# Macaron attention on one core: the order of the work beside the first unit's maxima, and beside the last heads' copies

## The chip, the core and the metric

The kernel runs on one core of a Trainium2 chip. The metric is the device time of one execution in microseconds (us), and the median over the runs is taken. The engines are called as in the profile: PE multiplies matrices, PEld is its weight load, DVE, ACT and POOL work on vectors, and SP issues most of the DMAs. All data is float32.

## What is computed

The input x has 8 batches of 1024 tokens with 256 features. The reference is a macaron block:

```
x = x + 0.5 * ffn(layernorm(x))
x = x + attn(layernorm(x))
x = x + 0.5 * ffn(layernorm(x))
```

`attn` is causal attention with 16 heads of 16 features: q, k and v are projections with biases, the scores q·k/4 get a causal mask and a softmax, and the weighted values go through the output projection Wo with bias bo. `ffn` sends each token to its two best of 8 experts, and an expert that is asked by more tokens than its capacity (1280 of 8192 tokens, where 2048 are the mean) gives nothing to anyone. The kernel counts the tokens of each expert, proves that none is kept, and runs a feed-forward path only if a count says otherwise. The trace shows no instruction of that path, so with these inputs both feed-forward layers add zero. What the time consists of is therefore the attention of 8 batches, the gate logits of both layers, the choice of two experts for each token, and the counts.

## The kernel before

**Units.** `attention` (from line 681 on) cuts the work into 32 units: unit u is batch u // 4 with group u % 4 of four heads. The four heads lie on partitions 0, 32, 64 and 96 of four rotating pairs of tiles qT and kT. The softmax is done in two passes. `m_steps(u)` multiplies q and k of unit u block by block (PE writes PSUM tiles named sm) and takes row maxima on DVE. `settle(u, hf)` sends the maxima of one half of the rows through DRAM (top_d) into row 16 of each head in qT, against a row of -1 in kT, so that the second multiplication comes out with the maximum already subtracted. `e_steps(u)` does that second multiplication (PSUM tiles sc), ACT takes the exponential into pT, POOL cuts the diagonal blocks, and PE multiplies by the values into pav. Six PSUM tiles serve sm and sc in rotation (`score`), and two more (`bank`) serve everything else.

**The main loop.** For u from -1 to 31 the loop does 24 steps. For u from 0 to 30, a step is two blocks of sc of unit u and two blocks of sm of unit u+1, and then the value products that are owed from earlier steps. For u = -1 there are no scores yet: 12 pairs of steps do only the maxima of unit 0, four blocks each. In the text P1 to P12 are these pairs, 512, 384, 256 and 128 columns wide in P1 to P4 and in P9 to P12, and 512 in P5 to P8.

**Work beside it.** All else is written as generators and handed to an object `Beside` (line 52). A generator yields PIECE before a piece of PE work, REST before the second half of a piece, or a number of steps to wait. `beside.step(True)` moves the clock on by one step, runs what is due, and then runs the open second half or opens one PIECE. So one call gives PE about half a piece of other work behind a step. `finish` runs a generator to its end at once. In the opening (u = -1) one `step` is called behind each pair. The order in which the Python calls are made is the order on each engine, since `InOrder` (line 27) chains the instructions of PE, DVE, ACT and POOL. SP's DMAs are not chained by it.

The generators that matter here:
- `weights` (line 215): turns the weight matrices with PE transposes, one piece for each of wk, wq, the gate, wv and wo. Then it centres the gate's weights (three DVE operations on gsb to gcs), turns them (pt_gc), multiplies them with bo and Wo (pg), and multiplies the bias of v by Wo (pb_v), whose result DVE adds to bo_all. Two copies on POOL, bo_cols and bv_cols, serve these products.
- `values_of(b, apart, j0, j1)`: a tile of v for 128 tokens in two halves (pv), copied by ACT to vaug and by DVE to the logits.
- `project(u, apart)`: q and k of units u and u+1, in four pieces of two halves (pq), one for each of k and q in each half of the tokens. ACT writes packed, and SP spreads it with 8 DMAs a piece, 32 in all, one for each head.
- `residual`, `gate_first`, `prepare`, `enter`: the residual with its bias on POOL, the first layer's choice of experts on DVE, and the next batch's layer norm.
- `leave_last(b, hf, pav, copies)`: the last four heads of the last batch. Two copies bring pav to SBUF (att_last), PE transposes, DVE divides (normed), PE transposes back (on_last), two copies follow, and four px_last products end it. `regate` then computes the second layer's logits and its choice of experts, about 20 small DVE operations, and `fewest` counts.

**Order around the change, before.** In the opening: the gate and wv behind P1, and values of tiles 0 to 3, half a tile behind each of P3 to P10. Nothing is left for P11 and P12. In unit 0, one half behind each step: values of tiles 4 to 7 (steps 0 to 7), `project(2)` (steps 8 to 15), then the rest of `weights`, then `residual(0)` and `gate_first(0)`. At the end, after the last unit: `finish` runs everything that is pending, which is the rest of the first half's `regate`, then the first layer's count, and only then `leave_last` for the second half.

Of the kernel before, what the change touches and what calls it, by code (L numbers as in the profile page):

```python
# [10 lines left out]
F32 = mybir.dt.float32  # L11
# [7 lines left out]
P = 128  # L19
# [29 lines left out]
PIECE, REST = "piece", "rest"  # L49
# [51 lines left out]
def macaron_kernel(  # L101
# [22 lines left out]
    DC = D // P  # L124
# [90 lines left out]
    def weights(pool, bank, matmul, transpose):  # L215
        def load(src, queue):
            wsb = pool.tile([P, DC, D], F32, tag="wsb", name="wsb", bufs=4)
            queue.dma_start(out=wsb, in_=src.rearrange("(c p) d -> p c d", p=P))
            return wsb

        wks, wqs = load(Wkv[:D], nc.scalar), load(Wq, nc.scalar)
        with nc.allow_non_contiguous_dma(reason="two vectors of 256"):
            for src, dst in ((bkv[:D], bkT), (bq, bqT)):
                nc.scalar.dma_start(out=dst, in_=src.rearrange("(c p) -> p c", p=P))
        gsb = const.tile([E, D], F32, name="gsb")
        nc.sync.dma_start(out=gsb, in_=gate_w)
        wvs, wos = load(Wkv[D:], nc.sync), load(Wo, nc.sync)
        nc.sync.dma_start(out=bo_all[:, :D], in_=bo.partition_broadcast(P))
        boT = const.tile([P, DC], F32, name="boT")
        bvT = const.tile([P, DC], F32, name="bvT")  # L230
        with nc.allow_non_contiguous_dma(reason="two vectors of 256"):
            nc.sync.dma_start(out=boT, in_=bo.rearrange("(c p) -> p c", p=P))
            nc.sync.dma_start(out=bvT, in_=bkv[D:].rearrange("(c p) -> p c", p=P))

        gpsimd.tensor_scalar(bqT, bqT, QSCALE, None, ALU.mult)

        def turn(wsb, dst):
            pt = bank("pt_w")
            for kc in range(DC):
                for oc in range(DC):  # L240
                    transpose(pt[:, kc * D + oc * P : kc * D + (oc + 1) * P], wsb[:, oc, kc * P : (kc + 1) * P])
            scalar.copy(dst, pt.rearrange("p (c d) -> p c d", c=DC))

        turn(wks, wkT)
        yield PIECE
        turn(wqs, wqT)
        yield PIECE
        pt = bank("pt_gate")
        for c in range(DC):
            transpose(pt[:, c * E : (c + 1) * E], gsb[:, c * P : (c + 1) * P], n=E)  # L250
        scalar.copy(gwT, pt[:, : DC * E].rearrange("p (c e) -> p c e", c=DC))
        yield PIECE
        turn(wvs, wvT[:, :, :D])
        yield PIECE
        turn(wos, woT[:, :, :D])
        yield PIECE
        mean = const.tile([E, 1], F32, name="g_mean")
        vector.tensor_reduce(mean, gsb, AX.X, ALU.add)
        vector.tensor_scalar(mean, mean, 1.0 / D, None, ALU.mult)
        gcs = const.tile([E, D], F32, name="gcs")  # L260
        vector.tensor_scalar(gcs, gsb, mean, None, ALU.subtract)
        pt = bank("pt_gc")
        for c in range(DC):
            transpose(pt[:, c * E : (c + 1) * E], gcs[:, c * P : (c + 1) * P], n=E)
        gcT = const.tile([P, DC, E], F32, name="gcT")
        scalar.copy(gcT, pt[:, : DC * E].rearrange("p (c e) -> p c e", c=DC))
        bo_cols = const.tile([P, DC, P], F32, name="bo_cols")
        gpsimd.tensor_copy(bo_cols, boT.unsqueeze(2).to_broadcast([P, DC, P]))
        bv_cols = const.tile([P, DC, P], F32, name="bv_cols")
        gpsimd.tensor_copy(bv_cols, bvT.unsqueeze(2).to_broadcast([P, DC, P]))  # L270
        yield PIECE
        pg = bank("pg")
        for oc in range(DC):
            matmul(pg[:, :E], bo_cols[:, oc], gcT[:, oc], start=(oc == 0), stop=(oc == DC - 1))
        for kc in range(DC):
            for oc in range(DC):
                matmul(
                    pg[:, (1 + kc) * E : (2 + kc) * E],
                    wos[:, oc, kc * P : (kc + 1) * P],
                    gcT[:, oc],  # L280
                    start=(oc == 0),
                    stop=(oc == DC - 1),
                )
        scalar.copy(bo_all[:, D:], pg[:, :E])
        scalar.copy(woT[:, :, D:], pg[:, E : (1 + DC) * E].rearrange("p (c e) -> p c e", c=DC))
        yield PIECE
        pb = bank("pb_v")
        for c in range(DC):
            matmul(pb[:, : D + E], bv_cols[:, c], woT[:, c], start=(c == 0), stop=(c == DC - 1))
        vector.tensor_tensor(bo_all, bo_all, pb[:, : D + E], ALU.add)  # L290
# [390 lines left out]
    def attention(run_no, src, dst, gate0, logits, tally):  # L681
# [3 lines left out]
        with stack:  # L685
# [491 lines left out]
            for kT in kTs[2:]:  # L1177
                scalar.copy(kT, row16.to_broadcast([P, S]))
            beside = Beside()
            opening = beside.add(chain(some(turning, 2), values_of(0, 0, 0, HT)))  # L1180
            owed, light, last, ons = deque(), deque(), [], {}
            STEPS = 24

# [1 line left out]
            for u in range(-1, NU):  # L1185
                b, g = divmod(u, NG)
                if u == 0:
                    beside.finish(opening)
                    beside.add(chain((PIECE,), turning, residual(0), gate_first(0)))
                    preparing = beside.add(prepare(1))  # L1190
                if u >= 0 and g == 0:
                    projecting = beside.add(project(u + 2, 3 if b else 1), first=True)
                if u == 0:
                    opening = beside.add(values_of(0, 0, HT, TB), first=True)
                if u >= 0 and g == 1:
                    beside.finish(projecting)
                if u >= 0 and g == 2 and b + 1 < B:
                    beside.finish(entering)
# [11 lines left out]
                for k in range(0, STEPS, 2) if u < 0 else ():  # L1210

                    for h in range(2):
                        ms[k](h)
                        ms[k + 1](h)
                    if k == 8:
                        beside.add(settle(0, 0), first=True)
                    beside.step(True)
                for k in range(0, STEPS, 2) if u == NU - 1 else ():

                    then = es[k + 1][1]  # L1220
# [20 lines left out]
                for k in range(STEPS) if 0 <= u < NU - 1 else ():  # L1241


                    scores, then = es[k]
                    for h in range(2):
                        scores(h)
                        if ms[k] is not None:
                            ms[k](h)
                    now = u * STEPS + k
                    if then is not None:  # L1250
                        owed.append((now + 2, then, 0))
                        owed.append((now + 3, then, 1))
                    while owed and owed[0][0] <= now:
                        _, then, part = owed.popleft()
                        then(part)
                    if light:
                        light.popleft()()
                    if u == NU - 2 and k in (0, 3):
                        beside.add(leave_first(b, k // 3))
                    if u == NU - 2 and k == 9:  # L1260
                        dividing = beside.add(divided(b, 0, 8, 12, ons[0][:, 1], (2, 3, 3, 3)))
                    if g == 3 and k == 9:

                        beside.add(leave(b, 0))
                    if g == 0 and b and k == 9:

                        beside.add(gate_first(b))
                    if g == 0 and b and k == 2:
                        beside.add(chain(leave(b - 1, 1), regate(b - 1, 0, TB)))
                    if g == 1 and k == 7 and b + 1 < B:  # L1270

                        beside.finish(preparing)
                        entering = beside.add(enter(b + 1), first=True)
                    if u == 0 and k == 15:
                        beside.finish(opening)
                    if k == 9 and ms[k] is not None:
                        beside.add(settle(u + 1, 0), first=True)
                    if k == 0:
                        settling = beside.add(settle(u, 1), first=True)
                    if k == 6:  # L1280
                        beside.finish(settling)
                    beside.step(k in long_steps or u == 0 or beside.pending() > 1)
            while owed:
                _, then, part = owed.popleft()
                then(part)
            while beside.works:
                beside.finish(beside.works[0])
            leasts = [None if gate0 is None else fewest("0", gate0[1], bank("cnt0"))]
            drain(leave_last(B - 1, 1, last.pop(), (scalar.copy, vector.tensor_copy)))
            drain(regate(B - 1, HT, TB))  # L1290
            leasts.append(fewest("1" if gate0 else "1b", tally, bank("cnt1")))
            for e in (pe, vector, scalar, gpsimd):
# [60 lines left out]
```

## Time and profile before

| | |
|---|---|
| median of 3 runs | 1412.6 us (1409.44 to 1412.75) |
| the profiled execution | 1412.56 us, its span 1410.7 us |
| PE busy | 1373.3 us (97%) |
| DVE busy | 1032.9 us (73%) |
| ACT busy | 788.5 us (56%) |
| POOL busy | 399.0 us (28%) |
| mean granted clock of PE | 0.983 |
| the chain that ended last | PE 93%, DVE 3%, POOL 2%, issue 1% |

The profile comes from one execution. A page of it gives the busy time of each engine, the span in 40 slices with the clock that PE was granted, the chain of work that ended last, and the costliest groups of instructions. The trace behind it can be asked for stretches: a timeline lists instructions merged into runs, with their start, their length and, in square brackets, the idle time of the engine before them and what ended it. A stretch of 2 us in the table of windows has the busy time and the number of instructions of each engine, and then PEclk, the granted clock as a share of full speed. Almost all instructions carry line 37, that of the helper that records them, so one goes by the names of the tiles. A matmul counts as two in the profile, and the ends of PE's records are modelled: a PE that waits with a started instruction shows as busy.

### The profile page before, as it was taken

To read this page: it belongs to the slowest core of one execution; us is meant where nothing else is said; L and a number is where in the kernel's file an instruction comes from. 1 tells how busy PE (TensorE), PEld (TensorE's weight loads), DVE (VectorE), ACT (ScalarE), POOL (GpSimd) and SP (SyncE) were. 2 spreads that over 40 slices of the span, in tenths; PEclk is the share of its full clock that TensorE was granted. 3 is DMA by queue.
4 is the path that set the end of the run, shared out by engine and by line. 5 is a ranking of instruction groups with operands and counts; after the bars stand their busy time and mean duration, and the time that the engine had idled before them with its cause. 6 is when DMAs were issued, how large, how long until landed. Compare 5 with 4: busy or idle time off the path is not lost.

```text
span 1410.7 us, 37948 instructions
## 1 busy us (share of the span) xinstructions
PE 1373.3 (97%) x14520; PEld 526.3 (37%) x14520; DVE 1032.9 (73%) x3417; ACT 788.5 (56%) x1790; POOL 399.0 (28%) x720
## 2 busy tenths in 40 slices
PE   7999999999999999999999999999999999999994
PEld 3334333343433333343333433334333333334431
DVE  4757677876778868777677777787677786778854
ACT  3246555555655656555555556555665565655561
POOL 3015114241143412352131421424114331222221
PEclk9889999999999999999999999999999999999997
DMA  4010101212111210212112121122111111121100
GB/s 146 10 40 26 41 25 50 57 61 72 34 54 60 73 44 29 78 49 71 40 35 70 43 87 32 48 65 69 52 32 58 55 47 41 42 65 63 42 26 33
DMA packets 66966, 72.85 MB, mean 52 GB/s; under 512 B 24688, under 2 KB 42232, under 8 KB 66776
## 3 DMA queue, kind: packets, MB, share of 16 engines
q1 hardware_dynamic: 65688, 69.82, 16.4%
q8 instruction: 116, 1.90, 0.5%
q14 instruction: 74, 0.61, 0.1%
q10 hardware_dynamic: 1088, 0.53, 0.1%
HBM read 26.87 MB, written 26.20 MB: 38 GB/s over the span
## 4 chain that ended last, share of the span: by engine, by line
PE 93%; DVE 3%; POOL 2%; issue 1%; DMA 0%; ACT 0%; ACTq 0%; POOLq 0%
PE sc L37 43%; PE pav L37 23%; PE pq L37 8%; PE sm L37 8%; PE pv L37 4%; PE px L37 4%; PE pta L37 1%; DVE sm L37 1%; POOL rstd_a L37 1%; POOL xa L37 1%; DVE first L37 0%; DMA bqT<-in_L_attn_bq_dram 0%; POOL pT L37 0%; PE px_last L37 0%; PE pg L37 0%
## 5 line engine op out<-in xcount | busy, mean ns | idle before, releaser
L37 ACT ACTIVATE pT<-sc 128x512 f32<-128x512 f32 (+3 forms) x1536 | 668.9, 488 | 533.3 <-PE sm L37 437.9
L37 PE MATMUL sm<-kT,qT 32*128 32x512 f32 (+3 forms) x3072 | 786.1, 537 | 0.2
L37 PE MATMUL sc<-qT,kT 32*128 32x512 f32 (+3 forms) x3072 | 735.2, 534 | 0.3 <-ACT pT L37 0.3
L37 POOL TENSOR_SCALAR_AFFINE_SELECT pT<-pT 128x256 f32<-128x256 f32 x512 | 208.0, 409 | 943.7 <-ACT pT L37 940.7
L37 DVE TENSOR_REDUCE first<-sm 128x1 f32<-128x512 f32 x512 | 328.5, 684 | 145.9 <-PE sm L37 143.9
L37 PEld LDWEIGHTS sc<-qT,kT 32*128 32x128 f32 x3072 | 258.2, 183 | 352.0 <-ACT pT L37 267.1
L37 PE MATMUL pav<-pT,vaug 128*32 128x256 f32 (+2 forms) x5120 | 386.2, 370 | 2.9 <-POOL pT L37 2.8
L37 DVE CUSTOM_DVE_ANT_0 sm<-sm,causal,first 128x256 f32<-128x256 f32 (+3 forms) x512 | 262.4, 556 | 80.1 <-PE sm L37 72.0
L37 PEld LDWEIGHTS sm<-kT,qT 32*128 32x128 f32 x3072 | 297.4, 184 | 22.7 <-DVE top L37 8.6
L37 DVE CUSTOM_DVE_ANT_0 sm<-sm,causal 128x256 f32<-128x256 f32 (+3 forms) x512 | 241.7, 515 | 85.6 <-PE sm L37 68.9
L37 PEld LDWEIGHTS pav<-pT,vaug 128*32 128x32 f32 x5120 | 103.7, 108 | 333.2 <-issue 219.1
L37 DVE DVE_READ_ACCUMULATOR2_ANT top<- 128x1 f32 x1024 | 145.2, 142 | 0.0
L37 PE MATMUL pv<-wvT,xnT 128*32 128x264 f32 x1024 | 83.7, 400 | 0.0
L37 PE MATMUL px<-woT,on 128*32 128x264 f32 x960 | 76.1, 389 | 0.0
L37 PE MATMUL pq<-xnT,wkT 128*32 128x512 f32 x512 | 68.4, 610 | 1.4 <-ACT xnT L37 1.4
L37 POOL TENSOR_SCALAR xn_a<-xa,mv_a,rstd_a 128x256 f32<-128x256 f32 x56 | 67.9, 1224 | 1.9 <-PE pta L37 1.0
L37 PE MATMUL pq<-xnT,wqT 128*32 128x512 f32 x512 | 67.4, 601 | 0.0
L37 POOL TENSOR_TENSOR on<-on,inv 128x512 f32<-128x512 f32 (+1 forms) x32 | 40.9, 1277 | 13.7 <-DMA inv<-inv_d 13.7
L37 PEld LDWEIGHTS pv<-wvT,xnT 128*32 128x32 f32 x1024 | 29.0, 111 | 41.5 <-issue 23.4
L37 POOL TENSOR_TENSOR xa<-xa,bo_all 128x528 f32<-128x528 f32 x32 | 41.8, 1306 | 0.6
L37 PEld LDWEIGHTS px<-woT,on 128*32 128x32 f32 x960 | 27.9, 109 | 33.5 <-issue 10.6
L37 ACT COPY vaug<-pv 128x256 f32<-128x256 f32 x64 | 24.4, 381 | 26.2 <-PE pv L37 25.2
(126 smaller groups left out, 482.6 us busy)
## 6 DMA issues: line engine op xcount, KB each, us to landing
att_d<-att SPq DMA_DIRECT2D x62, 256.0 KB
kT<-packed SPq DMA_DIRECT2D x256, 32.0 KB
qT<-packed SPq DMA_DIRECT2D x256, 32.0 KB
out_dram<-xa SPq DMA_DIRECT2D x16, 512.0 KB
on<-att_d SPq DMA_DIRECT2D x30, 256.0 KB
inv<-inv_d SPq DMA_DIRECT2D x30, 256.0 KB
xa<-in_L_attn_x_dram SPq DMA_DIRECT2D x7, 1024.0 KB
xa<-in_L_attn_x_dram SPq DMA_DIRECT2D x2, 512.0 KB
```

The lines of the kernel that those rows point to most:

```text
L37: i = call(*args, **kwargs)
```

## The change

Four edits:
- In the opening, two calls of `step` instead of one follow each pair, and the opening's list is longer: after the values of tiles 0 to 3 come all of `project(2)` (with `apart` 0, no waits between the pieces) and the rest of `weights`. With two calls the halves of a piece stand together, 24 halves in all behind 12 pairs.
- In `weights`, the small DVE operations and the two POOL copies are moved ahead of a wait of two steps and a PIECE.
- In unit 0, only the values of tiles 4 to 7 and the preparation of batch 1 are left from the start; `residual(0)` and `gate_first(0)` are added at step 15.
- At the end, the steps of `Beside` run only while PE work is open or pending. Then `leave_last` begins: its two copies come first, and three steps of the first half's `regate` follow each of its first two parts, the first layer's count with the second; the rest goes behind the third part.

```diff
         turn(wos, woT[:, :, :D])
-        yield PIECE
         mean = const.tile([E, 1], F32, name="g_mean")
...
         vector.tensor_scalar(gcs, gsb, mean, None, ALU.subtract)
+        bo_cols = const.tile([P, DC, P], F32, name="bo_cols")
+        gpsimd.tensor_copy(bo_cols, boT.unsqueeze(2).to_broadcast([P, DC, P]))
+        bv_cols = const.tile([P, DC, P], F32, name="bv_cols")
+        gpsimd.tensor_copy(bv_cols, bvT.unsqueeze(2).to_broadcast([P, DC, P]))
+        yield 2
+        yield PIECE
         pt = bank("pt_gc")
...
-            opening = beside.add(chain(some(turning, 2), values_of(0, 0, 0, HT)))
+            opening = beside.add(chain(some(turning, 2), values_of(0, 0, 0, HT), project(2, 0), (PIECE,), turning))
...
                 if u == 0:
                     beside.finish(opening)
-                    beside.add(chain((PIECE,), turning, residual(0), gate_first(0)))
                     preparing = beside.add(prepare(1))
-                if u >= 0 and g == 0:
-                    projecting = beside.add(project(u + 2, 3 if b else 1), first=True)
-                if u == 0:
                     opening = beside.add(values_of(0, 0, HT, TB), first=True)
-                if u >= 0 and g == 1:
+                if u > 0 and g == 0:
+                    projecting = beside.add(project(u + 2, 3), first=True)
+                if u > 1 and g == 1:
                     beside.finish(projecting)
...
-                    beside.step(True)
+                    for _ in range(2):
+                        beside.step(True)
...
                     if u == 0 and k == 15:
                         beside.finish(opening)
+                        beside.add(chain(residual(0), gate_first(0)))
...
-            while beside.works:
-                beside.finish(beside.works[0])
-            leasts = [None if gate0 is None else fewest("0", gate0[1], bank("cnt0"))]
-            drain(leave_last(B - 1, 1, last.pop(), (scalar.copy, vector.tensor_copy)))
+
+            while beside.open is not None or beside.pending():
+                beside.step(True)
+            leasts = [None]
+            for k, _ in enumerate(leave_last(B - 1, 1, last.pop(), (scalar.copy, vector.tensor_copy))):
+                for _ in range(3 if k < 2 else len(beside.works) * STEPS):
+                    beside.step(False)
+                if k == 1 and gate0 is not None:
+                    leasts = [fewest("0", gate0[1], bank("cnt0"))]
```

More of the change, by code (lines that the diff above doesn't have):

```diff
@@ L266, in weights @@
         scalar.copy(gcT, pt[:, : DC * E].rearrange("p (c e) -> p c e", c=DC))
[L267 to L270, printed above, removed]
         yield PIECE
```

## The prediction, made before the changed kernel ran

> **What bounds the kernel now.** I read the 40 slices first.
>
> ```profile
> PE   7999999999999999999999999999999999999994
> PEclk9889999999999999999999999999999999999997
> ```
>
> PE is full except at both ends, and only there is its clock cut, so the places that the change touches are where time can be had. Then the windows of 2 us (start:end, length, then busy time and number of instructions of PE, PEld, DVE, ACT and POOL, then PEclk) over the first 140 us:
>
> ```profile
> 30.00:32.00 2.00, 2.00 (x18) 1.01 (x17) 2.00 (x11) 0.00 (x0) 0.00 (x0) 0.96 0.22 53
> 34.00:36.00 2.00, 2.00 (x7) 1.41 (x8) 0.26 (x2) 0.30 (x1) 0.00 (x0) 0.50 0.24 56
> 60.00:62.00 2.00, 2.00 (x16) 0.56 (x12) 1.55 (x5) 1.39 (x3) 0.41 (x1) 0.50 0.02 4
> 98.00:100.00 2.00, 2.00 (x14) 2.00 (x10) 0.62 (x2) 0.23 (x1) 0.41 (x1) 0.50 0.22 52
> ```
>
> All the windows together show the clock at half from about 31.9 to 42.1, 55.7 to 62.6 and 96.7 to 106.9 us (the ends from the mixed windows, such as the 0.96 here), and next only near the end. PE's "2.00 busy" in the second row holds 7 matmuls, where full windows hold 20 to 36: there it is waiting. Next the timelines, for where units begin and what stalls them:
>
> ```profile
> 54.30 0.69 PE L37 MATMUL sc<-qT,kT 32*128 32x512 f32 x1
> 112.23 0.69 PE L37 MATMUL sc<-qT,kT 32*128 32x512 f32 x1
> 90.96 0.66 PE L37 MATMUL pt_w<-ident,wsb 128*128 128x128 f32 x4 [0.82 <-ACT packed L37]
> 95.72 0.20 PE L37 MATMUL pt_gc<-ident,gcs 8*128 8x8 f32 x1 [2.47 <-DVE gcs L37]
> 98.86 1.85 PE L37 MATMUL pg<-gcT,wsb 128*128 128x8 f32 x8
> 103.26 2.13 PE L37 MATMUL pb_v<-woT,bv_cols 128*128 128x264 f32 x4
> ```
>
> The first two lines are the first sc of unit 0 and of unit 1: the opening's maxima run from 25.3 to 54.3 us, unit 0 takes 57.9 us. Inside unit 0 PE waits 0.82 us for a bank and 2.47 us because the small gate operations stand behind the maxima on DVE.
>
> **What the Trainium skill says.**
> - "TensorE: Matmul & The Clock Gate", part "What's actually happening": PE's clock is halved after an idle window of about 3.4 us and comes back after a busy one, and the window runs free of the kernel. The trace agrees: the three cuts last 10.2, 6.8 and 10.2 us, three, two and three such windows, each after a thin stretch. The page gives no share of busyness that counts as idle, so I bound that below.
> - "DMA: Bandwidth & Descriptors", part "Anatomy of one DMA": about 2 us fixed for a small transfer. The trace agrees: the store of the maxima is issued at 57.74 us and the load that needs it at 59.74.
> - "PSUM — Partial Sum Buffer", part on bank collisions: two engines on one bank are kept apart, reads too. The trace agrees: DVE's second on copy shows an idle time that ends with ACT's copy of the other half (1.27 us, most of it the common wait for PE).
>
> **Part 1, what unit 0 loses.** A step with half a projection (pq) beside it and one without:
>
> ```profile
> 78.65 0.64 PE L37 MATMUL pav<-pT,vaug 128*32 128x256 f32 x8
> 81.14 0.64 PE L37 MATMUL pav<-pT,vaug 128*32 128x256 f32 x8
> 139.77 0.64 PE L37 MATMUL pav<-pT,vaug 128*32 128x256 f32 x8
> 143.46 0.64 PE L37 MATMUL pav<-pT,vaug 128*32 128x256 f32 x8
> ```
>
> From pav to pav it is 2.49 us with pq, and (143.46 - 139.77) / 2 = 1.85 us without: half a projection is 0.97 us of PE, but only 0.65 comes back, since plain steps partly wait for exponentials and maxima. Second half of unit 0 now: 112.23 - 71.16 (its first sc) = 41.1 us. Off come 8 x 0.65 = 5.2; pt_w 0.6; the waits 0.8 + 2.5; pt_gc 0.2; pg 2.7 and pb_v 2.05 (start to next start, at half clock); and half of the other 5.2 us under the half clock, 2.6. Left: 24.4 us. First half: 71.16 - 57.82 (second step) = 13.3 us, of which 4.75 at half clock, so 11.0 at full clock. Unit 0 after the change: 35.4 us, plus about 0.5 for a wait at its start (my estimate; it is some 1.4 us now), plus half of whatever half-clock time falls into it.
>
> **Part 2, what the opening gains.** At full clock PE needs for four sm blocks 1.05 us (512 wide), 0.85 (384), 0.62 (256), 0.41 (128); a value tile 1.16; a projection piece 1.94; pt_w 0.6. DVE needs 0.62 to 0.67 us for each 512 block, so 2.5 to 2.7 a pair. P5 can't end before the second half of q has landed: SP issues unit 0's four DMAs of it until 34.0 us, about 2 us later the last one is there, and the last block follows: 36.75. From there PE has value tile 3, 1.16; P6 to P9 with a piece each, 4 x 3.0 (DVE's 2.5 fits beneath); P10 and pt_w 1.45; P11 0.6. That is 51.9 us. pt_gc waits for gcs: DVE ends P9 at about 50.2, P10 2.1 later (four blocks of 0.52), gcs and what leads to it take 0.9 (0.37, 0.14, 0.34): 53.3. Then pt_gc and its copy 0.4; pg 1.4 (half of 2.7); P12 0.4 and the copies 0.6; pb_v 1.0: 57.1, minus little overlap, about 56.7. P10 to P12 are as thin as what precedes the cut at 55.7 today, so I take pb_v at half clock: unit 0 starts at 58.0 instead of 54.3. The cover for the moved work is that PE idles under DVE's maxima; without the cover the whole 7.8 (pq) + 0.8 + 1.4 + 1.0 = 11.0 us is added (case D).
>
> Other queues: ACT's four packed and four copies find it nearly idle in the opening. The POOL copies (0.40 each) wait only for loads of 8 us. `residual` and `gate_first` keep their work. The 32 head DMAs now stand on SP ahead of the store of unit 0's second-half maxima:
>
> ```profile
> 57.74 0.55 SPq L897 DMA_DIRECT2D top_d<-turned  x1
> 59.74 0.49 SPq L899 DMA_DIRECT2D qT<-top_d  x1
> 77.00 4.99 SPq L850 DMA_DIRECT2D kT<-packed  x8
> 88.21 6.03 SPq L850 DMA_DIRECT2D kT<-packed  x8
> ```
>
> Eight take 4.95 to 6.03 us, 0.67 each on the mean of the four groups. The first packed ends at about 36.75 + 1.16 + 1.05 + 1.94 + 0.7 (ACT) = 41.6: 41.6 + 32 x 0.67 = 63.0, plus 2 + 2 for store and load: 67. Step 8 of unit 0 needs it at 58.0 + 0.5 + 11.0 + 2.3 = 71.8. No stall, with under 5 us to spare.
>
> **Part 3, the end.**
>
> ```profile
> 1384.84 0.37 ACT L37 COPY att_last<-pav 128x256 f32<-128x256 f32 x1 [1.26 <-PE pav L37]
> 1387.55 0.42 DVE L37 COPY att_last<-pav 128x256 f32<-128x256 f32 x1
> 1387.59 1.14 PE L37 MATMUL pt_last<-ident,att_last 128*128 128x128 f32 x4 [2.82 <-DVE counts L37]
> 1388.76 0.26 DVE L37 RECIPROCAL inv_last<-pt_last 128x16 f32<-128x16 f32 x1 [0.72 <-PE pt_last L37]
> ```
>
> The DVE copy can start after ACT's, at 1385.25. But in the changed order eight small operations (0.22 us each, start to start) stand between it and the reciprocal: 1385.67 + 8 x 0.22 = 1387.4 instead of 1388.76. The rest of the small operations and the count (about 1.8 us) fit under on_last, its copy and the first px_last. So 1.3 us, not the 2.3 that the copy itself comes earlier; bounds 0.5 (they do not fit) and 2.5 (the clock stays full, so on_last and the products shorten too).
>
> **The sum (case A).** Half clock in unit 0 until 62.6 as now: (62.6 - 58.0) / 2 = 2.3. Unit 1 starts at 58.0 + 35.4 + 0.5 + 2.3 = 96.2 instead of 112.2: 16.0 us. With 1.3 at the end, 17.3. From the profiled execution's 1412.56 us (1.9 above its span; 0.04 under the median): 1395.3 us.
>
> **The rivals.**
> - B, the fuller opening keeps the clock up throughout: 56.7 + 35.9 = 92.6, 19.6 + 1.3 saved: 1391.7. For it: pairs P6 to P9 with half a tile behind them hold full clock today. Against: P11 and P12 stay thin.
> - C, the cut at 31.9 us comes all the same, as P3 to P5 still wait for DVE and for q: P5 ends at 37.5, value tile and P6 run at half clock to 41.9, and all is 3 us later: 1398.3.
> - D, PE is really as full in the opening as the page says, and the moved work costs its full 11.0 us: unit 0 starts at 65.3, unit 1 at 101.2: 11.0 + 1.3 saved, 1400.3. Against: 7 matmuls in 2 us.
> - E, the slower one: the 32 DMAs hold back the load of the maxima. It decides from (71.8 - 45.6) / 32 = 0.82 us each. At 1.5 us each, over the longest single one seen (1.29), the load lands at 93.6, a stall of 21.8 us, more than is saved: 1417.
> - That the work is not moved is out: the compiled instruction order shows it behind the pairs.
>
> **Chances.** A 0.42, B 0.17, C 0.25, D 0.12, E 0.04. The low end is B less most of the 3.1 us by which the fastest run shown lies under the median, 1389.0; the high end is D with one more window of half clock (1.7 us), 1402.0. A measurement of this kernel can tell about 0.3%, 4.2 us, from no change. Faster by more: A, B, C and all of D but 0.02: 0.94. Within: that 0.02 and half of E: 0.04. Slower: the other half of E: 0.02.
>
> **What would show it.** Right: unit 1's first sc at 93 to 99 us; no pq, pt_w, pg or pb_v between the first sc and it; plain steps of 1.85 us; the store of the second-half maxima issued near 63 us, with no wait of sc for qT; the reciprocal of the last heads about 1.3 us nearer to the last pav. Wrong: unit 0 starting after 62 us (D), sc of step 8 waiting for a DMA (E), half clock where I have none, or a longer stretch from unit 1 on, where I take nothing to change.

## The result and the profile after

| | before | after |
|---|---|---|
| median (6 runs each) | 1412.57 us (1409.44 to 1413.68) | 1397.82 us (1396.69 to 1398.7) |
| the profiled execution | 1412.56 us, span 1410.7 | 1397.34 us, span 1395.5 |

The ratio is 0.9898, with a 95% interval from 0.9885 to 0.9911: 14.75 us saved, where 17.3 were forecast. The time lies inside the range, 2.5 us above the forecast.

PE's row of slices hardly differs (the first slice reads 6 where it read 7). The clock's row does: the second and third slice read 9 where they read 8.

```profile
PE   6999999999999999999999999999999999999994
PEclk9999999999999999999999999999999999999997
```

The windows of 2 us (columns as in the prediction), the four shown of before and 54 to 56:

```profile
30.00:32.00 2.00, 2.00 (x40) 1.02 (x28) 2.00 (x14) 0.37 (x1) 0.00 (x0) 1.00 0.23 57
34.00:36.00 2.00, 2.00 (x14) 0.86 (x18) 1.42 (x3) 0.00 (x0) 0.00 (x0) 1.00 0.21 50
54.00:56.00 2.00, 2.00 (x13) 1.98 (x16) 0.06 (x2) 0.17 (x2) 0.00 (x0) 0.50 0.22 53
60.00:62.00 2.00, 2.00 (x20) 0.82 (x16) 1.47 (x5) 1.08 (x2) 0.42 (x1) 0.99 0.22 53
98.00:100.00 2.00, 2.00 (x17) 0.82 (x14) 1.35 (x8) 0.76 (x2) 1.23 (x3) 1.00 0.01 4
```

The first window holds 40 matmuls where it held 18, and the cut at 31.9 us is gone, as is the one at 96.7. One stretch at half clock is left. Its length comes from the clock of each window: 0.80 in 52 to 54 means 0.8 us at half, then three full windows, then 0.99: 6.8 us in all, against 27.3 us before.

The timeline of PE has the moved work in the opening and the starts of unit 0 and unit 1:

```profile
37.70 1.92 PE L37 MATMUL pq<-xnT,wkT 128*32 128x512 f32 x16
40.63 1.92 PE L37 MATMUL pq<-xnT,wqT 128*32 128x512 f32 x16
52.53 0.26 PE L37 MATMUL pt_gc<-ident,gcs 8*128 8x8 f32 x2 [1.28 <-DVE gcs L37]
53.15 0.94 PE L37 MATMUL pg<-gcT,bo_cols 128*128 128x8 f32 x4 [0.35 <-ACT gcT L37]
53.94 1.85 PE L37 MATMUL pg<-gcT,wsb 128*128 128x8 f32 x8
56.46 2.13 PE L37 MATMUL pb_v<-woT,bv_cols 128*128 128x264 f32 x4
58.52 1.22 PE L37 MATMUL sc<-qT,kT 32*128 32x512 f32 x1
60.90 0.69 PE L37 MATMUL sc<-qT,kT 32*128 32x512 f32 x1
78.79 0.64 PE L37 MATMUL pav<-pT,vaug 128*32 128x256 f32 x8
82.36 0.64 PE L37 MATMUL pav<-pT,vaug 128*32 128x256 f32 x8
98.02 0.69 PE L37 MATMUL sc<-qT,kT 32*128 32x512 f32 x1
```

A pair with a projection piece takes 40.63 - 37.70 = 2.93 us. The plain step is (82.36 - 78.79) / 2 = 1.79 us. Unit 1 begins at 98.02 instead of 112.23. The first sm of this execution is at 24.05 us (25.29 before), because its loads were there sooner, so 1.24 of these 14.21 us are no part of the change. SP's queue, the store and the load of the second-half maxima:

```profile
63.77 0.58 SPq L898 DMA_DIRECT2D top_d<-turned  x1
65.79 0.51 SPq L900 DMA_DIRECT2D qT<-top_d  x1
```

Step 8 of unit 0, which needs them, begins at 72.44 us with no wait. From unit 1 on the two timelines run side by side, 14.2 us apart at first and 13.83 at the last scores. Then the end:

```profile
1370.66 0.37 ACT L37 COPY att_last<-pav 128x256 f32<-128x256 f32 x1 [0.91 <-PE pav L37]
1371.06 0.42 DVE L37 COPY att_last<-pav 128x256 f32<-128x256 f32 x1 [0.46 <-ACT att_last L37]
1371.08 0.90 PE L37 MATMUL pt_last<-ident,att_last 128*128 128x128 f32 x4 [0.50 <-ACT att_last L37]
1373.05 0.25 DVE L37 RECIPROCAL inv_last<-pt_last 128x16 f32<-128x16 f32 x1
1374.10 1.04 PE L37 MATMUL on_last<-ident,normed 128*128 128x128 f32 x4 [1.95 <-DVE cand_g L37]
```

From ACT's copy to the reciprocal it is 2.39 us where it was 3.92. DVE has no idle time ahead of the reciprocal: the small operations stand there, as the prediction said.

### The profile page after: what moved, and what is told of

It reads as the page before. It is cut to its first block, busy times and chain, and to the rows that moved or that the text cites. A ratio compares the mean times of both kernels' runs of the same rounds, so it can differ in the third digit from the quotient of the medians.

```text
span 1395.5 us, 37945 instructions
## 1 busy us (share of the span) xinstructions
PE 1359.8 (97%) x14520; PEld 523.1 (37%) x14520; DVE 1032.8 (74%) x3417; ACT 788.4 (56%) x1790; POOL 399.1 (29%) x720
## 4 chain that ended last, share of the span: by engine, by line
PE 93%; DVE 3%; POOL 2%; issue 1%; DMA 1%; ACT 0%; ACTq 0%; SPq 0%; DVEq 0%; POOLq 0%
PE sc L37 43%; PE pav L37 23%; PE pq L37 8%; PE sm L37 8%; PE pv L37 4%; PE px L37 4%; PE pta L37 1%; DVE sm L37 1%; POOL rstd_a L37 1%; POOL xa L37 1%; DMA bqT<-in_L_attn_bq_dram 0%; POOL pT L37 0%; PE px_last L37 0%; PE pg L37 0%; DVE sums L37 0%
## 5 line engine op out<-in xcount | busy, mean ns | idle before, releaser
L37 PE MATMUL sm<-kT,qT 32*128 32x512 f32 (+3 forms) x3072 | 777.9, 533 | 1.1 <-DVE top L37 0.8
L37 PE MATMUL pv<-wvT,xnT 128*32 128x264 f32 x1024 | 80.6, 389 | 0.0
L37 POOL TENSOR_TENSOR on<-on,inv 128x512 f32<-128x512 f32 (+1 forms) x32 | 40.9, 1277 | 12.8 <-DMA inv<-inv_d 12.8
L37 PEld LDWEIGHTS px<-woT,on 128*32 128x32 f32 x960 | 27.9, 109 | 33.6 <-issue 10.6
L37 ACT COPY att<-pav 128x512 f32<-128x512 f32 x62 | 36.7, 592 | 0.0
```

What stands on the lines that cost most here:

```text
L37: i = call(*args, **kwargs)
```

## The experiments

Two lengths are read from each trace: the opening (first sm to first sc) and unit 0 (its first sc to unit 1's). The column "at half clock" has the time at half clock within both, from the clocks of the windows.

| kernel | opening | unit 0 | sum | at half clock | median, and before beside it |
|---|---|---|---|---|---|
| before | 29.0 | 57.9 | 86.9 | 27.3 | 1412.6 |
| after | 34.5 | 39.5 | 74.0 | 6.8 | 1397.8 (1412.6) |
| e1_proj | 28.1 | 49.5 | 77.7 | 13.7 | 1402.9 (1409.5) |
| e2_weights | 30.9 | 46.7 | 77.6 | 10.2 | 1403.2 (1409.5) |
| e3_end | 29.3 | 55.3 | 84.6 | 20.5 | 1408.4 (1409.5) |
| e4_one | 39.9 | 47.2 | 87.1 | 23.9 | 1410.4 (1409.5) |
| c_after | 34.4 | 39.7 | 74.1 | 6.8 | 1397.4 (1409.7) |
| e5_gate | 31.4 | 39.9 | 71.3 | 3.4 | 1394.5 (1409.7) |
| e6_order | 30.7 | 50.2 | 80.9 | 17.1 | 1404.3 (1409.7) |
| e9_later | 33.1 | 39.5 | 72.6 | 6.8 | 1395.5 (1409.7) |
| e10_mix | 32.8 | 39.5 | 72.3 | 3.4 | 1395.9 (1412.3) |
| e11_end | 30.1 | 42.1 | 72.2 | 6.8 | 1394.3 (1412.3) |
| e12_both | 34.1 | 39.5 | 73.6 | 6.8 | 1396.1 (1412.3) |

The theory is that of the prediction: PE idles under DVE's maxima in the opening, so work put there is covered. The rivals are D (PE is full there, the work costs its whole 11.0 us) and E (the head DMAs hold back the load of the maxima).

**Only the projections moved (e1_proj), against the kernel before:**

```diff
-            opening = beside.add(chain(some(turning, 2), values_of(0, 0, 0, HT)))
+            opening = beside.add(chain(some(turning, 2), values_of(0, 0, 0, HT), project(2, 0)))
...
-                    beside.step(True)
+                    for _ in range(2):
+                        beside.step(True)
```

(and no `project(2)` in unit 0)

> Only the projections of units two and three move into the opening, with two calls of step behind each pair; the rest of the weights stays in unit 0, and the end is as before. Cover theory (PE idles under DVE's maxima in the opening, so moved work is nearly free until that idle time is used up): opening from the first sm to the first sc about 28 us, as before (29.0), unit 0 about 50.5 us instead of 57.9; about 8 us faster than before, 1404. Rival D (PE is really full in the opening, moved work costs its full time): the opening grows by 7.8 us and unit 0 shrinks by 5.2; 2 to 3 us slower than before, 1415.

Measured: 1402.87 us, ratio 0.9951 (0.9934 to 0.9967). e3_end, on the same chip and with the opening and unit 0 of the kernel before, is the fitting yardstick: 84.6 - 77.7 = 6.9 us. The opening is not longer but 1.2 us shorter with 7.8 us more of PE work in it, since the cut at 31.9 is gone. That is cover, not D. It is not full cover: a microsecond at half clock cost about 0.35 us (worked out further below), so the 10.2 us of the cut were worth some 3.6, and by this estimate about 2 of the 7.8 us were not covered. In unit 0 the gate's products stayed behind, with their wait (1.89 us, 2.47 before), and the cut behind it stayed too, 6.8 us long (clock 0.83 in the window from 76 to 78):

```profile
75.61 0.20 PE L37 MATMUL pt_gc<-ident,gcs 8*128 8x8 f32 x1 [1.89 <-DVE gcs L37]
```

**Only the rest of the weights moved (e2_weights), against the kernel before:**

```diff
-            opening = beside.add(chain(some(turning, 2), values_of(0, 0, 0, HT)))
+            opening = beside.add(chain(some(turning, 2), values_of(0, 0, 0, HT), (PIECE,), turning))
```

(with two steps per pair, and the changed order in `weights`)

> Only the rest of the weights moves into the opening (with two calls of step); the projections stay in unit 0, and the end is as before. Cover theory: opening about 29 us as before, unit 0 loses pt_w 0.6, the waits 3.3, pt_gc 0.2, pg 2.7, pb_v 2.05 and the half clock that follows them 2.6, so 11.5 us faster than before, 1401; together with the projections alone that is more than the whole change gives, since both share one stretch of idle time. Rival D: the opening grows by 3.2 us of PE work, so 8.3 us faster, 1404, and the two parts add up to less than the whole.

Measured: 1403.22 us, ratio 0.995 (0.9933 to 0.9967), 7.0 us less in opening and unit 0. That is less than the cover theory said. The median lies 6.2 us under that of before, less than the 11.5 of the cover theory and less than the 8.3 of D too, so the time alone doesn't decide between them; the lengths do better. Unit 0 is 8.6 us shorter, but the opening 1.6 longer: the values are done by P5, P6 to P8 held only the thin pieces, with a wait of pt_gc for gcs of 1.03 us, and the clock fell from about 45 us on.

```profile
44.00:46.00 2.00, 2.00 (x17) 1.28 (x16) 1.09 (x2) 0.24 (x2) 0.00 (x0) 0.75 0.00 0
46.00:48.00 2.00, 2.00 (x9) 0.99 (x4) 1.13 (x2) 0.00 (x0) 0.00 (x0) 0.50 0.03 8
48.00:50.00 2.00, 2.00 (x15) 1.05 (x13) 1.87 (x5) 0.00 (x0) 0.00 (x0) 0.90 0.00 0
```

The parts add up to more than the whole: alone they save 6.9 + 7.0 = 13.9 us in opening and unit 0, together (c_after) 84.6 - 74.1 = 10.5. The opening tells where the rest is: -1.2 and +1.6 us alone, +5.1 together. The medians agree with less force: 6.6 + 6.2 = 12.8 us for the parts, and 12.3 - 1.1 = 11.2 for the whole without its end, a difference within their noise. I read this as one budget of cover that two users share; the clock has a part in it, since 4.4 us at half clock lie in c_after's opening and 0.6 in e1_proj's.

**Only the end (e3_end):** the last hunk of the change on the kernel before.

> Only the end is changed (the last heads' copies sooner). The reciprocal moves by 1.3 us against the last value product, so 1411.2, about 1.3 us faster than before. A rival: the small operations only change places on a DVE that is busy throughout, 0 to 0.5 us.

Measured: 1408.4 us, ratio 0.999 (0.9981 to 1.0): 1.1 us. The interval reaches from nothing to 2.7 us, so the time can't tell the 1.3 us expected from the 0 to 0.5 of the rival. The traces can: from the start of the last pav products to the start of the last DVE operation it is 18.7 us here and 20.5 before. In all eight kernels with this end it is 18.6 to 19.0 us, in the three with the old one 20.3 to 20.5.

**The whole change with one step per pair (e4_one), against the changed kernel:**

```diff
-                    for _ in range(2):
-                        beside.step(True)
+                    beside.step(True)
```

What does not fit behind the pairs then runs in one lump ahead of unit 0.

> The whole change, but with one call of step behind each pair: what doesn't fit behind the pairs runs in one lump between the maxima and unit 0, without cover. Cover theory: about 7 of the 8 halves of the projections and all of the rest of the weights stand after P12, some 12 us of PE, so the opening takes about 41 us instead of 34.5, 1404. Rival D (there is no cover): the same as the whole change, 1398.

Measured: 1410.43 us, ratio 0.9997 (0.9987 to 1.0008), worse than both theories said. The opening is 39.9 - 29.3 = 10.6 us longer, nearly the 11.0 us that case D took for uncovered work. And unit 0 met what rival E describes:

```profile
78.80 0.63 PE L37 MATMUL pv<-wvT,xnT 128*32 128x264 f32 x8
82.80 1.19 PE L37 MATMUL sc<-qT,kT 32*128 32x512 f32 x1 [3.38 <-DMA qT<-top_d]
```

```profile
78.35 0.58 SPq L898 DMA_DIRECT2D top_d<-turned  x1
80.38 0.51 SPq L900 DMA_DIRECT2D qT<-top_d  x1
```

The projections ended later, so the head DMAs and the store behind them on SP came at 78.35 us instead of 63.77. The wait of 3.38 us is followed by 10.2 us at half clock. Against c_after unit 0 is 7.5 us longer, over twice the wait.

**The gate's operations first (e5_gate), with the changed kernel beside it (c_after):** the centring of the gate's weights and the two POOL copies are moved ahead of the first pair.

```diff
             for kT in kTs[2:]:
                 scalar.copy(kT, row16.to_broadcast([P, S]))
+            next(turning, None)
```

(with the generator's DVE and POOL operations moved up to this point, and its wait of two steps gone)

> The changed kernel itself once more, as the yardstick for the three kernels beside it. Ratio to the kernel before 0.990 as measured at first; opening (first sm to first sc) 34.5 us, unit 0 (first sc to unit 1's first sc) 39.5 us, half clock from about 53.5 to 60.3 us.

> The three DVE operations that centre the gate's weights, and the two POOL copies, run before the first pair instead of behind P10. If the wait of pt_gc for gcs (1.28 us) is what opened the last half-clock stretch and what made my opening 1.8 us too short, the wait goes, pg runs at full clock and the whole is 1.5 to 3 us faster than the changed kernel. If the clock falls there in any case because P11 and P12 are thin, and the wait is only changed for another (DVE's maxima), it is at most 0.5 us faster.

Measured: c_after 1397.39 us, ratio 0.9911 (0.9895 to 0.9927); e5_gate 1394.49 us, ratio 0.9891 (0.9874 to 0.9908). The medians differ by 2.9 us and the openings by 34.4 - 31.4 = 3.0, so the time is where the wait was:

```profile
50.61 0.22 PE L37 MATMUL pt_gc<-ident,gcs 8*128 8x8 f32 x1
52.01 0.61 PE L37 MATMUL pg<-gcT,bo_cols 128*128 128x8 f32 x4
52.48 1.04 PE L37 MATMUL pg<-gcT,wsb 128*128 128x8 f32 x8
53.89 1.66 PE L37 MATMUL pb_v<-woT,bv_cols 128*128 128x264 f32 x4 [0.38 <-issue]
```

pt_gc waits for nothing, and pg runs at full clock. The wait of 1.28 us was worth more than its length, and that holds with less luck in the clock too: e11_end below has the same instructions there and one more window at half clock, and its opening and unit 0 are still 1.9 us shorter than c_after's.

**The weights ahead of the projections (e6_order), and the same with 16 heads' DMAs later (e9_later):**

```diff
-            ... values_of(0, 0, 0, HT), project(2, 0), (PIECE,), turning))
+            ... values_of(0, 0, 0, HT), (PIECE,), turning, project(2, 0)))
```

In e9_later the DMAs of unit 3's heads are kept in a list and issued in unit 0 after the store of the second-half maxima.

> As the one before, and the weights' pieces stand ahead of the projections in the opening, so that P9 to P12 hold the dense projection pieces. If thin work at the opening's end is what cuts the clock, the opening runs at full clock to its end and is 3 to 5 us shorter than the changed kernel's 34.5. But the head DMAs start some 4 us later on SP: 45.5 + 32 x 0.67 + 4 = 71, while step 8 of unit 0 then wants the maxima at 53 + 14 = 67 or so. If SP's queue stands on that path as my rival E said, sc of step 8 waits 2 to 5 us for the load of the maxima, and little of the gain is left (0 to 2 us in all). If it does not, the whole is 4 to 5 us faster than the changed kernel.

> As the one before, but the 16 head DMAs of unit 3 are issued only after the maxima of unit 0's second half have been sent off (step 6 of unit 0), so that 16 instead of 32 stand ahead of them: 45.5 + 16 x 0.67 + 4 = 60, before step 8 wants them. If SP's queue is what costs in the kernel beside it, the wait at step 8 is gone here and the whole is 3 to 5 us faster than the changed kernel; if the two are equal, the queue was not on the path.

Measured: e6_order 1404.28 us, ratio 0.9956 (0.9942 to 0.9969); e9_later 1395.48 us, 0.9899 (0.9882 to 0.9915). The two differ only in when 16 DMAs are issued. e6_order, PE and SP:

```profile
74.56 1.19 PE L37 MATMUL sc<-qT,kT 32*128 32x512 f32 x1 [4.65 <-DMA qT<-top_d]
```

```profile
70.49 0.58 SPq L898 DMA_DIRECT2D top_d<-turned  x1
72.54 0.51 SPq L900 DMA_DIRECT2D qT<-top_d  x1
```

In e9_later the store is issued at 67.17 us, and step 8 begins at 72.66 with no wait:

```profile
67.17 0.58 SPq L901 DMA_DIRECT2D top_d<-turned  x1
72.66 0.69 PE L37 MATMUL sc<-qT,kT 32*128 32x512 f32 x1
```

Its unit 0 is 50.2 - 39.5 = 10.7 us shorter. So SP's queue is on the path as soon as the projections are later or unit 0 is earlier, and the wait of 4.65 us cost 10.7, with 17.1 us of half clock from 72.6 us on. Both expectations missed in size: against c_after e6_order lost 6.9 us where 0 to 2 were to be gained, and e9_later gained 1.9 of 3 to 5. That e9_later gained no more than e5_gate is the clock: in its profile 6.8 us at half clock lie in the opening from 42.8 us on, under work that ran at full clock in e6_order's.

**The thin pieces among dense ones (e10_mix), the end once more (e11_end), and both (e12_both), all on e5_gate:**

```diff
-            opening = beside.add(chain(some(turning, 2), values_of(0, 0, 0, HT), project(2, 0), (PIECE,), turning))
+            rest = project(2, 0)
+            opening = beside.add(
+                chain(some(turning, 2), values_of(0, 0, 0, HT), some(rest, 7), some(turning, 4), rest, (PIECE,), turning)
+            )
```

```diff
-            for k, _ in enumerate(leave_last(B - 1, 1, last.pop(), (scalar.copy, vector.tensor_copy))):
-                for _ in range(3 if k < 2 else len(beside.works) * STEPS):
+            for k, _ in enumerate(leave_last(B - 1, 1, last.pop(), (scalar.copy, scalar.copy))):
+                for _ in range((0, 3, 0)[k] if k < 3 else len(beside.works) * STEPS):
...
-                if k == 1 and gate0 is not None:
+                if k == 3 and gate0 is not None:
```

> As the kernel with the gate's operations ahead of the pairs (opening 31.4 us, unit 0 39.9 us, half clock 54.8 to 57.7 us, 1394.5 us), but the thin pieces (pt_w, pt_gc, pg, pb_v) stand behind P9 and P10 and the fourth projection piece behind P11 and P12, so that no two pairs in a row at the opening's end are thin. If it is the thin end that has the clock cut, the stretch at half clock goes and 1 to 2 us come off opening and unit 0 together. If windows of PE are cut by where they fall and not by how thin this end is, the stretch is there again, a little earlier, and the time is the same within 0.5 us. The queue of head DMAs is not longer: when the fourth piece is ready at about 53 us, the first 24 heads keep SP busy until about 58.

> As the kernel with the gate's operations ahead of the pairs (1394.5 us), and at the end both copies of the last heads on ACT, the division right behind their transpose, and only then the steps of regate and the count. In the changed kernel eight small DVE operations of 0.22 us stand ahead of the reciprocal (it starts 2.3 us after the last pav's first copy ends). If DVE is the engine that bounds the last heads, two copies of 0.42 us leave it and the reciprocal comes up to 1.5 us sooner, but the small operations still have to be done before the last logits: 0.4 to 1.0 us less in all. If PE at half clock and the chain on_last, copy, px_last bound it, 0 to 0.3.

> Both edits of the two kernels beside it together: the sum of what each of them gains over 1394.5 us, 1392 us if both do what their first theories say, 1394 if neither.

Measured: e10_mix 1395.94 us, ratio 0.989 (0.9873 to 0.9908); e11_end 1394.3 us, 0.9877 (0.9859 to 0.9896); e12_both 1396.13 us, 0.989 (0.9872 to 0.9907). The intervals overlap each other and e5_gate's; e12_both was to take 1392 or 1394 us. My first theory for e10_mix fell: its opening has the cut again, one window of it, sooner and under denser work:

```profile
52.00:54.00 2.00, 1.62 (x6) 1.34 (x6) 1.35 (x6) 0.24 (x2) 0.00 (x0) 0.64 0.21 51
54.00:56.00 2.00, 2.00 (x10) 0.20 (x8) 0.43 (x1) 0.00 (x0) 0.00 (x0) 0.50 0.20 49
```

The thin stretch is only at another place (P9 and P10). And e12_both, with the same instructions in its opening, has a second cut there, 3.4 us long, that begins under P5's waits and the value tile behind them:

```profile
34.00:36.00 2.00, 2.00 (x18) 0.79 (x21) 1.41 (x3) 0.00 (x0) 0.00 (x0) 0.98 0.20 49
36.00:38.00 2.00, 2.00 (x16) 0.69 (x12) 1.07 (x4) 0.37 (x1) 0.00 (x0) 0.50 0.24 57
```

Its opening is 1.3 us longer than e10_mix's. For e11_end, the last heads did go faster at first:

```profile
1371.25 0.26 DVE L37 RECIPROCAL inv_last<-pt_last 128x16 f32<-128x16 f32 x1 [1.23 <-PE pt_last L37]
1371.91 0.63 PE L37 MATMUL on_last<-ident,normed 128*128 128x128 f32 x4 [0.70 <-DVE normed L37]
1376.48 1.99 PE L37 MATMUL px_last<-woT,on 128*32 128x264 f32 x16 [0.75 <-DVE counts L37]
```

The reciprocal comes 2.8 us after the start of the last pav products instead of 4.0. But the small DVE operations now hold up the third px_last, and from pav to the last operation it is 18.5 us, against 18.7 in c_after and 19.4 in e12_both. No gain can be told there; the likely reason, not tested, is that DVE has the same work ahead of the same end. e11_end has the lowest ratio of all kernels run, but nothing tells it from e5_gate.

## Why the prediction was nearly right

- **Cover (case A against D): right.** e1_proj puts 7.8 us of PE work into an opening that gets shorter; e4_one takes the cover away, and the opening grows by 10.6 us.
- **The cut at 31.9 (case C): right that it goes, but by a narrow margin.** It is there in e4_one and e3_end, with one step per pair, and gone in nine of the ten kernels with two steps. The tenth is e12_both, which gives PE the same work up to there as the changed kernel: a cut of 3.4 us came at 35.9. So C was a real risk, and that the measured executions escaped it is partly luck; the last section estimates how near it was.
- **P5 to P9: right.** The first pq was to start at 36.75 + 1.16 + 1.05 = 38.96 us; with the earlier start of that execution, 37.72; it was 37.70. Pairs of 3.0 us took 2.93.
- **The end of the opening: too short by 1.8 us.** I gave it 3.7 us over before, it took 5.5. The failed step is "pg 1.4 (half of 2.7)": the clock fell at about 53.2 us, not at P12, and pg took 0.94 + 1.85 us. I had the wait for gcs (its end at 53.3 us; it was 52.39, or 53.6 with the 1.24 us of the later start), but counted only its length and not what it does to the clock. e5_gate takes it away and gets 3.0 us.
- **First half of unit 0: right by luck.** 13.8 us were forecast and 13.9 measured (72.44 - 58.52), but two errors cancel. The sum began at the second step (57.82) and put only 0.5 us, for a wait, in place of the first, which takes 2.4 (58.52 to 60.90). And it counted 2.3 us for 4.6 us at half clock, of which only 1.5 us came (58.5 to 60.0), with no cost to be seen: e9_later, with no half clock in unit 0, takes 13.9 us as well (72.66 - 58.77).
- **Second half of unit 0: too short by 1.2 us.** 24.4 forecast, 98.02 - 72.44 = 25.6 measured, and 25.6 again in c_after, e5_gate and e9_later. The plain step was right (1.79 for 1.85). What failed is the way, a sum of subtractions: the eight steps with pq (71.16 to 90.07 us before, 72.44 to 86.49 after) gave back 4.85 us instead of 5.2, and the rest 10.6 instead of 11.45. Part of the latter is "half of the other 5.2 us under the half clock": the kernel before and e3_end have the same instructions up to unit 1, with 27.3 and 20.5 us at half clock, and differ by 2.4 us; a microsecond at half clock cost 0.35 us there, not 0.5. With that, 0.8 of the 1.2 us are accounted for. No run tests this share alone, but the 42 runs of the kernel before that stand beside e1_proj to e4_one give the same price: a line through their spans and mean clocks rises by 1.03 us for each 0.001 of clock lost, which is 2.8 us at half clock, so 0.36 us each. The length was to be read without any sum: the second half of unit 1, which has no projection, is 154.35 - 129.11 = 25.2 us in the trace of before, by the stores of the maxima.
- **The queue on SP (rival E): right about the kernel, wrong about its price.** The store was forecast "near 63", it came at 63.77, and the load landed about 4.6 us ahead of need. Kernels with 32 DMAs a little later fell over that edge (e4_one, e6_order), and paid 2.2 to 2.3 times the wait, where I had counted it once.
- **The end: right.** 1.3 forecast; the spans differ by 15.2 us, of which 13.8 were there at the last scores: 1.4.

In sum: 17.3 - 1.8 (end of the opening) - 1.2 (second half) + 1.24 (earlier start) - 0.4 (lost again by the last scores) + 0.1 (the end) = 15.2 us, the difference of the spans. The 1.24 us are luck of one execution; without them the forecast would lie 3.3 us above that difference.

How much the change saves depends also on the kernel before: 14.75 us beside a median of 1412.6, 12.3 beside 1409.7. Its third cut can make a difference of that size: 10.2 us long in the profiled execution, 3.4 in e3_end's, where unit 1 starts 2.4 us sooner after the first sm. The 17.3 us were worked out from an execution with the long cut, the one that leaves more to save.

## What to carry to other kernels

Work that PE can do beside another engine's bound stage was nearly free here until the gaps were full; so sum the moved work against the gaps, pair by pair, and try the parts alone and together. A wait on PE costs more than its length where it lets the clock fall: here taking away 1.3 us gave 3.0, and 4.65 cost 10.7. A length that comes out as forecast is no proof of its terms, as the first half of unit 0 shows. If what is moved issues DMAs, find what stands behind them on their queue and by when it is due. And the length of a stretch without its extra work is better read from a like stretch later in the trace than worked out by subtraction.

## What the runs showed of the hardware that was not expected

All stretches at half clock in the openings and in unit 0 have lengths of 3.4, 6.8, 10.2 or 17.1 us: one, two, three or five times 3.4. The Trainium skill's page "TensorE: Matmul & The Clock Gate" (part "What's actually happening") gives that window and says that it is free-running. The runs agree, and show what that means for a comparison: e5_gate and e11_end have the same instructions up to the last heads, and one had 3.4 us at half clock there, the other 6.8. e11_end's windows, to be read by the column that is third from the right:

```profile
54.00:56.00 2.00, 1.87 (x14) 1.30 (x16) 0.92 (x6) 0.03 (x1) 0.00 (x0) 0.89 0.24 61
56.00:58.00 2.00, 2.00 (x8) 0.77 (x4) 1.47 (x9) 0.57 (x1) 0.00 (x0) 0.50 0.11 25
58.00:60.00 2.00, 2.00 (x14) 0.71 (x16) 1.05 (x5) 0.62 (x2) 0.42 (x1) 0.50 0.20 49
60.00:62.00 2.00, 2.00 (x16) 0.21 (x10) 0.35 (x1) 0.40 (x1) 0.00 (x0) 0.50 0.20 49
```

Opening and unit 0 took 71.3 us in the one and 72.2 in the other, and 72.3 in e10_mix against 73.6 in e12_both. So one window is worth 0.9 to 1.3 us there, and a single profile of such a kernel can't tell edits apart that gain less.

How full a window must be to keep the clock can be estimated from the traces. The cuts of one trace lie on one grid: before, they begin at 31.9, 55.8 and 96.7 us, and 23.9 and 64.8 us are 7 and 19 windows of 3.41. Give each matmul the time of its columns at the rate of the projections (16 of 512 columns, four side by side, in 1.72 us: e4_one, 56.76 to 58.48), and add this up in each window of the grid. In the 13 traces, from 24 to 1340 us, the 22 windows just ahead of a cut hold at most 37% of such work, and all other windows at full clock 38% or more. The two sides lie close together, so the bound is good to a few per cent only. In the last heads, after 1340 us, it fails: ten windows of 22 to 35% kept the clock. It was drawn from these traces afterwards and tested on no other kernel.

The estimate fits what the experiments left open. The window with P5's waits holds 39% in the changed kernel (32.7 to 36.1 us), which kept its clock, and 37% in e12_both (32.5 to 35.9), which did not. The same thin pieces in the same place were cut in e9_later, where the grid put most of them into one window (39.4 to 42.8, 29%), and not in e6_order, where two windows shared them (38.4 to 45.3, 53 and 45%). Windows full of projections are far from the bound: they hold 82 to 88% in the changed kernel (36.1 to 49.8 us).
